# Copies of states with the step moved to the write, the last tokens' features in other PSUM banks, weights turned ahead of a scan, and a new order of 1534 pieces

## The chip, the cores and the metric

The kernel runs on one core of one Trainium2 chip. The time is device microseconds of one launch. PE is the matrix engine (PEld its loads of weights), DVE the vector engine, ACT the scalar engine, POOL the GpSimd engine, SP the engine that issues most DMAs. SBUF is the on-chip memory of 128 partitions; PSUM holds the results of PE in banks of 512 fp32 per partition.

## The reference

The input `x` is (4, 32, 128, 128) in fp32: 4 batches, 32 images ("tokens"), 128 rows `h` of 128 elements. Two layers follow each other; each adds a mixing part and then a recurrent part to `x`. `_ln_c` and `_ln_t` normalise each row of 128.

```python
# --- layer 0 ---
x = x + _L0_conv_ref(_ln_c(x), ...)     # attention over the 32 tokens with spectral convolutions, two mixers
t = _to_tokens(x)                       # (4, 32*128, 128): rows one after the other
t = t + _L0_ffn_ref(_ln_t(t), W, V, gamma, beta)
x = _from_tokens(t, x)
# --- layer 1 ---
x = x + _L1_conv_ref(_ln_c(x), bias, up_filter, dn_filter)
t = _to_tokens(x)
t = t + _L1_ffn_ref(_ln_t(t), W, V, gamma, beta)
x = _from_tokens(t, x)

def _ffn_ref(x, W, V, gamma, beta):     # the same for both layers
    Wx = einsum('bti,hi->bth', x, W)    # then batch norm over all B*T rows
    y[t] = sigmoid(Wx[t] + y[t-1] @ V.T)    # a scan over the 4096 rows of a batch

def _L1_conv_ref(x, bias, up, dn):      # every image by itself
    x = x + bias                        # one per token
    x = repeat(x, 2, both axes); x = conv_same(x, up)    # 12 x 12 taps, separable
    x = leaky_relu(x, 0.2) * sqrt(2)
    x = conv_same(x, dn)[::2, ::2]
```

## The kernel before

`XA` [128 rows h, batch, token, 128 w] holds the images in SBUF throughout. `WX` holds, for each group of 8 tokens, `[h, (token, batch)]` columns with the 128 features on the partitions: first the products `W x`, then the states of the recurrence. The program has these stages, with their place in the profiled execution: the attention of layer 0 (0 to about 240 us), the mixers and the products of the first recurrence (to 485), the scan of layer 0 (485 to 541), the convolution of layer 1 together with what surrounds it (541 to 835), and the scan of layer 1 with the output (835 to 911).

**The recurrences.** `Recurrence(layer, ...)` turns its two 128x128 weights on PE when it is made (`ps_wt`, L408 and L409), and `prepare()` copies them to SBUF (L414). While tokens are multiplied (`ps_wx`, L446), DVE takes bn_stats of each product (L449) and ACT copies it to `WX` (L1671). `scan()` first combines these statistics (`bn_aggr`, L1895; POOL's power, L360; L1898, L1899) and then goes over the rows: the 32 tokens and 5 pieces of 26 rows of each are run side by side from a guessed state with 12 warming steps, each step a product (L1912), a DVE addition (L1913) and a sigmoid on ACT (L1914). `f0.check()` (`CK` in the list below) compares the ends of pieces with the starts of the next ones; a second, sequential program stands behind a flag for the case that they differ, and is not run here.

**The convolution stage** is one list of 1534 names, `CONVOLUTIONS`, written out in the source. A loop issues the pieces in the order of the list, and `in_order` ties the instructions of PE, DVE, ACT, POOL and SP to that order on each engine. So the list sets which work stands behind which on an engine; between engines only data and buffers make one wait for another. A piece is a name and a token `t` (0 to 31), with a batch where it has `t.b`, or a unit `u` (0 to 63: half a token, two batches):

- `YC t`: ACT copies the states of token t out of `WX` to `yc` (L2099); `Ya t`, `Yb t`: PE turns them in two rounds to `ps_y`; `A t`: DVE adds them to `XA` (L2102).
- `CS t`: row statistics for the norm ahead of the convolution (DVE, L385); `CN`, `CP`, `CO q`: for a group of tokens the variance (DVE, L2013 to L2018), its power on POOL (L2025), the shifts (DVE, L2031, L2036); `X t.b`: the normalised image `XN` (POOL, L2045; DVE and ACT, L2042, for tokens 0 and 1).
- `Ra u`, `Rb u`: PE filters up along one axis into `ps_r`; `Q u`: ACT copies to `q`; `Ka u`, `Kb u`: the other axis into `ps_k`; `La u`, `Lb u`: ACT copies to `raw` (L2172); `Va u`, `Vb u`: DVE's leaky relu to `U` (L2180).
- `D u`: PE filters `U` of unit u down one axis into `ps_d` (L2190) and the copied result of unit u-1 down the other into `ps_e` (L2197); `C u` and `E u`: ACT's copies of the two; `AD u`: the sum to `XA`, on POOL for odd u below 58 and on DVE for the others (L2213).
- `FS t`: row statistics of the finished token (DVE, L385) and a DMA of it to DRAM (`turned`, SP, L2118); `FN`, `FP`, `FO q`: as `CN`, `CP`, `CO`; `N t.b`: the normalised image `xn` (POOL; DVE and ACT for tokens 30 and 31); `Ta t`, `Tb t`: turned on PE into `ps_x`; `TC t`: ACT's copy to `xt` (L2131); `M t`: the products with W of the second recurrence into `ps_w` (PE, L2136); `PS t`: their bn_stats (DVE, L2140); `PC t`: ACT's copy to `WX` (L2144).

A pass with an `a` and a `b` part uses PE's quarters; the `b` part waits for a no-operation on SP (L2072) that waits for the `a` part, so SP's queue, with the DMAs of `FS`, stands between them. PSUM is shared out as `ps_r` one tile of two banks, `ps_d` one bank, `ps_e` one bank, and `ps_k` two tiles of two banks for `Y`, `K`, `T` and `M`. Of `yc`, `xn` and `xt` there are two buffers, of `XN` three. At the end of the stage DMAs read `turned` back into `XA` in another order (L2244, L2247), ahead of the output of the second scan.

## Time and profile before

| | |
|---|---|
| three runs | 911.6, 914.01, 912.22 us; median 912.22 |
| profiled execution | 912.8 us; span of its instructions 911.0 us |
| busy share of the span | PE 89%, PEld 67%, DVE 80%, ACT 74%, POOL 40% |
| mean granted clock of PE | 0.946 |
| first scan, 485 to 541 us | PE busy 52.30 of 56.00, clock 1.00 |
| start of the convolution stage, 541 to 560 us | PE busy 14.28 of 19.00, clock 0.55 |
| its middle, 560 to 815 us | PE busy 247.48 of 255.00, DVE 197.01, ACT 201.61, POOL 198.21, clock 1.00 |
| its end, 815 to 836 us | PE busy 16.87 of 21.00, clock 0.92 |

All durations are of one profiled execution. A group line gives the source line, engine, operation, output and input tiles with their shapes, the count, then the busy time in us and the mean in ns, then the idle time of the engine ahead of these instructions and what ended it. A timeline line gives the start and the length in us of one instruction, or of several that follow each other, and in brackets the idle time before it with its releaser.

### The profile page before, as it was taken

Reading aid. Unit: us, or ns where it says so; the run is one execution under the profiler, and the core shown is the slowest. Engines: PE = TensorE matmul, PEld = TensorE weight load, DVE = VectorE, ACT = ScalarE, POOL = GpSimd, SP = SyncE. Lnnn points to the kernel's source line nnn. Section 1 sums busy time; section 2 is a strip of 40 time slices with the busy share of each in tenths; the row PEclk is TensorE's granted clock in tenths of the full one; section 3 lists DMA queues with packets and bytes.
Section 4 is the critical chain, followed back from the end, with each engine's and each line's share of the span. In section 5 each row is a group of like instructions: output and inputs, shape, how many; then the busy total and the mean of one; then the engine's idle time right before and its main releaser. Section 6 shows DMA issues by size and latency. Waiting matters only on the chain.

```text
span 911.0 us, 31218 instructions
## 1 busy us (share of the span) xinstructions
PE 806.4 (89%) x12678; PEld 608.0 (67%) x12678; DVE 728.3 (80%) x2352; ACT 670.1 (74%) x1644; POOL 364.1 (40%) x605
## 2 busy tenths in 40 slices
PE   2999969998796899999778988999999999997994
PEld 2656557568673465555436986888878888884994
DVE  5997477778667889989988988887777787666996
ACT  2774636565672879998788996888778787775995
POOL 2000000003142554344521003687977977962253
PEclk9999979997767999999999997999999999999997
DMA  9906000000101101102100000111111111118354
GB/s 228 240 4 124 1 1 1 1 1 1 48 1 47 47 25 47 48 25 70 47 1 1 1 1 3 39 39 38 39 28 38 31 35 40 38 39 306 123 180 151
DMA packets 69419, 49.67 MB, mean 55 GB/s; under 512 B 4561, under 2 KB 64465, under 8 KB 69201
## 3 DMA queue, kind: packets, MB, share of 16 engines
q1 hardware_dynamic: 68929, 47.31, 18.2%
q8 instruction: 102, 1.67, 0.8%
q0 software_dynamic: 288, 0.01, 0.2%
q14 instruction: 52, 0.43, 0.2%
q10 hardware_dynamic: 48, 0.26, 0.1%
HBM read 30.68 MB, written 16.88 MB: 52 GB/s over the span
## 4 chain that ended last, share of the span: by engine, by line
PE 40%; DVE 24%; ACT 11%; POOL 8%; issue 4%; DMA 0%; DVEq 0%; SPq 0%; ACTq 0%; POOLq 0%
PE ps_k L2066 5%; PE ps_d L2190 4%; DVE XA L1584 4%; DVE XA L1583 4%; ACT WXY L1914 3%; PE ps_scan L1912 3%; ACT yw L1914 3%; PE ps_y L1303 3%; PE ps_r L2066 2%; PE pm L1055 2%; PE ps_w L2136 2%; PE ps_e L2197 2%; PE ps_st L1426 2%; PE ps_inv L481 2%; POOL c_r L2025 2%
## 5 line engine op out<-in xcount | busy, mean ns | idle before, releaser
L1913 DVE SCALAR_TENSOR_TENSOR ps_scan<-WXY,bs,ps_scan 128x128 f32<-128x128 f32 x376 | 104.8, 351 | 1.3 <-PE ps_scan L1912 0.8
L2180 DVE SCALAR_TENSOR_TENSOR U<-raw 128x512 f32<-128x512 f32 x128 | 87.5, 701 | 20.2 <-ACT raw L2172 19.9
L2066 PE MATMUL ps_k<-WXY,q 64*64 64x134 f32 x2048 | 86.7, 283 | 0.4
L2172 ACT COPY raw<-ps_k 128x512 f32<-128x512 f32 x128 | 73.3, 595 | 13.5 <-PE ps_k L2066 11.3
L2190 PEld LDWEIGHTS ps_d<-WXY,U 128*64 128x64 f32 x2048 | 67.4, 137 | 20.2 <-issue 14.4
L2045 POOL TENSOR_SCALAR XN<-XA,c_r,c_o 128x128 f32<-128x128 f32 x120 | 78.1, 664 | 1.2 <-PE ps_k L2066 0.7
L2190 PE MATMUL ps_d<-WXY,U 128*64 128x67 f32 x2048 | 73.4, 224 | 0.5 <-DVE U L2180 0.4
L2045 POOL TENSOR_SCALAR xn<-XA,f_r,f_o 128x128 f32<-128x128 f32 x120 | 62.8, 534 | 17.3 <-PE ps_x L2066 14.0
L2066 PEld LDWEIGHTS ps_k<-WXY,q 64*64 64x64 f32 x2048 | 60.7, 135 | 6.7 <-ACT raw L2172 1.1
L2066 PE MATMUL ps_r<-WXY,XN 64*64 64x134 f32 x1024 | 57.3, 285 | 5.5 <-POOL XN L2045 2.6
L850 PE MATMUL ps_st<-cst,XA 128*128 128x130 f32 x256 | 43.5, 310 | 14.3 <-ACT XA L833 11.2
L1641 ACT ACTIVATE xn<-XA,f_o,f_r 128x128 f32<-128x128 f32 x120 | 50.9, 489 | 4.7 <-DVE f_o L1623 4.6
L1420 ACT ACTIVATE Z<-Z,k,aB 128x128 f32<-128x128 f32 x128 | 51.1, 481 | 3.4 <-DVE Z L1415 3.2
L850 PEld LDWEIGHTS ps_st<-cst,XA 128*128 128x128 f32 x256 | 35.2, 206 | 27.4 <-ACT XA L833 12.3
L1583 DVE SCALAR_TENSOR_TENSOR XA<-ps_inv,r1B,xin 128x128 f32<-128x128 f32 x128 | 44.0, 344 | 8.7 <-PE ps_inv L1576 8.7
L1584 DVE SCALAR_TENSOR_TENSOR XA<-Z,gB,XA 128x128 f32<-128x128 f32 x128 | 46.5, 363 | 5.0
L2025 POOL TENSOR_TENSOR c_r<-c_e,neg_half 128x16 f32<-128x16 f32 (+2 forms) x10 | 25.8, 2582 | 52.6 <-DVE c_e L2018 52.5
L496 PE MATMUL ps_inv<-invq,cst 64*128 64x512 f32 x128 | 41.9, 685 | 4.5 <-ACT invq L487 3.8
L2158 ACT COPY q<-ps_r 128x512 f32<-128x512 f32 x64 | 37.9, 591 | 8.6 <-PE ps_r L2066 8.3
L1290 DVE TENSOR_TENSOR df<-WXY 128x1088 f32<-128x1088 f32 x32 | 40.2, 1286 | 2.1 <-PE ps_y L1303 2.1
L2197 PE MATMUL ps_e<-WXY,q 128*64 128x67 f32 x1024 | 40.8, 222 | 0.0
L446 PE MATMUL ps_wx<-xt,wvt 128*128 128x512 f32 x64 | 35.6, 640 | 5.8 <-ACT WXY L453 4.5
(459 smaller groups left out, 2249.0 us busy)
## 6 DMA issues: line engine op xcount, KB each, us to landing
XA<-in_x_dram SPq DMA_DIRECT2D x16, 512.0 KB, 7.3
xin<-in_x_dram SPq DMA_DIRECT2D x32, 256.0 KB, 3.3
turned<-XA SPq DMA_DIRECT2D x32, 256.0 KB, 2.5
out_dram<-res SPq DMA_DIRECT2D x52, 128.0 KB, 2.1
XA<-turned SPq DMA_DIRECT2D x6, 1024.0 KB, 9.5
WXY<-dd SPq DMA_DIRECT2D x4, 544.0 KB, 11.1
XA<-turned SPq DMA_DIRECT2D x6, 256.0 KB, 7.3
out_dram<-resl SPq DMA_DIRECT2D x12, 128.0 KB, 2.1
```

What stands on the lines that cost most here:

```text
L850: mm(p[:, i, :], XA[:, b, t0 + j + i, :], cst[:, C_E : C_E + 130], start=True, stop=True)
L1420: nc.scalar.activation(z, z, AF.Gelu, bias=k1, scale=aB[:, j : j + 1])
L1583: stt(a, p2[c, b][:, i], r1B[:, j : j + 1], xin[c, b - b % 2][:, b % 2, i], ALU.mult, ALU.add)
L1584: stt(a, Z[c][:, b, i], gB[c][:, n : n + 1], a, ALU.mult, ALU.add)
L1913: stt(p4, WX[:, :, h, :], s[:, 0:1], p4, ALU.mult, ALU.add)
L1914: nc.scalar.activation(dst, p4, AF.Sigmoid, bias=s[:, 1:2])
L2045: e.tensor_scalar(dst, src_, r, o, ALU.mult, ALU.add)
L2066: m = mm(dst, data, taps, start=(n == 0 and (i, j) not in last), stop=(n == 1), skip_group_check=True)
L2172: nc.scalar.copy(raw[u, k], banks["k", u][:, k])
L2180: stt(U[u][:, k].rearrange("p k s m -> p (k s m)"), v, SLOPE, v, ALU.mult, ALU.max)
L2190: mm(p[HALVES[s], m, b, REACH[k]], U[v][:, b, k, s, HALVES[m]], DR[:, k, REACH[k]], start=(m == 0 and b == 0 and k == 0), stop=(k == 1), s ...
L2197: mm(p[HALVES[j], b * P : b * P + P][:, REACH[m]], q3[v - 1][:, m, b, HALVES[j]], DC[:, m, REACH[m]], start=(b == 0 and m == 0), stop=(m = ...
```

## The change

Four things are changed. The first three are small:

```diff
-        f0.scan()
         with tc.tile_pool(name="ps_f", bufs=1, space=PSUM) as ps_f:
             f1 = Recurrence(1, xtp, wk, ps_f, ps_f)
             f1.prepare()
+        f0.scan()
-        H2 = NB // 2
+        H2, LATE = NB // 2, NT - 4
...
-                            banks[name, u] = pool.tile([P, 2, 4 * P], F32, tag="x", name=f"ps_{name}")
+                            banks[name, u] = pool(u).tile([P, 2, 4 * P], F32, tag="x", name=f"ps_{name}")
...
             def state_columns(t):
                 yc[t] = cv.tile([P, NB, P], F32, tag="yc", name="yc")
                 j = t % TP * NB
-                nc.scalar.copy(yc[t], WX[:, t // TP, :, j : j + NB].rearrange("p h b -> p b h"))
+                nc.scalar.copy(yc[t].rearrange("p b h -> p h b"), WX[:, t // TP, :, j : j + NB])
...
             def feature_products(t):
-                p = banks["w", t] = ps_k.tile([P, 2, 4 * P], F32, tag="x", name="ps_w")[:, 0]
+                if t < LATE:
+                    p = ps_k.tile([P, 2, 4 * P], F32, tag="x", name="ps_w")[:, 0]
+                elif t % 2:
+                    p = ps_d.tile([P, 2, H2, P], F32, tag="d", name="ps_w").rearrange("p m b h -> p (m b h)")
+                else:
+                    p = ps_e.tile([P, 4 * P], F32, tag="e", name="ps_w")
+                banks["w", t] = p
...
-                ("Y", "y", ps_k, turned_by(lambda t, w, b, h: yc[t][w, b, h])),
-                ("T", "x", ps_k, turned_by(lambda t, h, b, w: xn[t][h, b, w])),
-                ("R", "r", ps_r, up_rows), ("K", "k", ps_k, up_cols),
+                ("Y", "y", lambda t: ps_k, turned_by(lambda t, w, b, h: yc[t][w, b, h])),
+                ("T", "x", lambda t: ps_r if t >= LATE and t % 2 else ps_k, turned_by(lambda t, h, b, w: xn[t][h, b, w])),
+                ("R", "r", lambda u: ps_r, up_rows), ("K", "k", lambda u: ps_k, up_cols),
```

1. `YC` goes through `WX` in the order in which it is stored: it reads runs of 4 elements (16 bytes) at a step of 32 elements and writes to `yc` with a step of 128 elements. Before, it read single elements at a step of 32 and wrote runs of 128.
2. The products of tokens 28 to 31 go to the banks of `ps_d` (odd tokens) and `ps_e` (even ones), and the turns of tokens 29 and 31 to `ps_r`, in place of `ps_k`.
3. The second recurrence's weights are turned and copied ahead of the first scan. On PE the two transposes then stand between the last two groups of products of the first recurrence; on DVE the copy stands ahead of the `bn_aggr` that begins the scan.
4. `CONVOLUTIONS` is another order of the same 1534 pieces. It begins and ends like this:

```diff
-YC0 YC1 Ya0 Ya1 Yb0 Yb1 YC2 A0 YC3 A1 Ya2 CS0 Yb2 Ya3 YC4 A2 Yb3 CN0 YC5 Ya4 Yb4 CS1 CP0 YC7 A3 CO0 Ya5 CN1 Yb5 X0.0
-YC6 CP1 CS2 X0.1 X0.3 X0.2 Ra0 CO1 CS3 Rb0 Q0 A4 Ra1 CN2 Ka0 Rb1 X1.0 Kb0 CP2 Q1 A5 X1.3 X1.2 La0 Ka1 CS4 Lb0 Ra3
-CO2 Kb1 X1.1 Va0 Ya6 X2.0 Rb3 X3.0 CS5 Yb6 Q3 X2.3 La1 Vb0 X2.1 Ra2 X2.2 Va1 Rb2 Lb1 X3.2 D0 A6 Q2 X3.1 X3.3 Vb1 Ka2
-C0 CK Ra4 Kb2 D1 La2 Lb2 Va2 Ka3 E0 C1 Rb4 AD0 Kb3 Vb2 Ya7 CS6 Q4 D2 La3 Lb3 Va3 Ra5 E1 Vb3 Ka4 C2 AD1 Yb7 Rb5 YC8
+YC1 Ya1 YC0 Ya0 Yb1 A1 Yb0 A0 CS0 CN0 CP0 CS1 YC3 Ya3 Yb3 A3 YC2 Ya2 Yb2 CO0 X0.0 X0.1 YC4 X0.3 Ra0 CN1 A2 YC5 Ya4
+X0.2 CS2 CP1 CO1 Rb0 Q0 X1.0 X1.3 X1.1 Yb4 A4 X1.2 Ra1 Ka0 YC6 CS3 CN2 CP2 Rb1 Kb0 CS4 Q1 La0 Va0 Lb0 Ra3 Ka1 Vb0
+CO2 X2.0 X2.1 Rb3 Ya5 Kb1 Q3 La1 Lb1 Ra2 Yb5 A5 X3.0 X3.2 Rb2 D0 Q2 Ya6 Ka2 X3.3 X3.1 C0 Va1 Ra4 Vb1 Yb6 A6 CS6 YC7
+Kb2 La2 Lb2 Va2 Vb2 D1 C1 Ka3 Ya7 CS5 E0 Rb4 Kb3 La3 Lb3 Va3 Q4 Yb7 D2 Ka4 X2.3 X2.2 C2 Ra5 YC8 Kb4 A7 Vb3 Rb5 E1
...
-Vb63 Ta25 E61 Ta26 C62 AD61 Tb25 Tb26 TC25 N28.0 FS30 D63 N27.0 TC26 N28.1 FN8 N28.3 M25 N28.2 E62 C63 N27.3 AD62
-N27.2 Ta28 PC25 N27.1 D64 PS25 FP8 Tb28 E63 TC28 AD63 M26 N29.0 FO8 FS31 N29.2 M28 PC26 N29.1 FN9 N29.3 PC28 PS26
-FP9 PS28 Ta27 FO9 Tb27 Ta29 TC27 N30.0 N30.1 Tb29 N30.2 M27 N31.0 TC29 N31.1 N31.3 N31.2 M29 PS27 N30.3 PC27 PS29
-Ta30 PC29 Tb30 Ta31 TC30 Tb31 M30 TC31 M31 PC30 PS30 PC31 PS31
+C61 Tb26 La63 FP7 FO7 N28.0 Va63 Lb63 D62 Ta25 Tb25 N28.1 TC26 N27.0 N27.1 N28.2 N27.2 Vb63 E61 AD61 FS30 M26 PS26
+FN8 C62 TC25 M25 PC25 PC26 D63 E62 N28.3 Ta28 Tb28 AD62 N27.3 N29.0 N29.3 PS25 C63 D64 N29.2 TC28 Ta27 E63 AD63 FS31
+FN9 N29.1 M28 Tb27 TC27 PC28 Ta29 Tb29 TC29 FP8 FO8 N30.0 N30.1 M27 N30.2 N30.3 FP9 FO9 N31.0 N31.1 N31.2 N31.3 M29
+PS29 Ta30 Tb30 TC30 PS28 PC29 Ta31 Tb31 M30 PS30 TC31 PC27 M31 PC31 PS27 PC30 PS31
```

In the lines left out the pieces of a unit still follow each other in the same sequence; the distances between the producers (`X`, `N`, `AD`) and their users are others, and `CK` has moved from before `D1` to behind `D6`.

## The prediction

> **What bounds the kernel now.** I read the slices of the span first, then a table of stretches, the groups of instructions, and the timeline at the three places that the change touches. The slices put the convolution stage at 541 to 835 us (slices 24 to 37). The table gives, for each stretch, its length, the busy time of PE, PEld, DVE, ACT and POOL, the granted clock, the DMA share and GB/s:

> ```profile
> 541.00:560.00 19.00, 14.28 (x306) 10.98 (x308) 13.38 (x59) 11.86 (x16) 6.76 (x10) 0.55 0.01 3
> 600.00:625.00 25.00, 24.03 (x764) 20.35 (x754) 20.04 (x57) 19.84 (x38) 24.76 (x37) 1.00 0.12 36
> 725.00:750.00 25.00, 24.70 (x790) 21.05 (x788) 20.29 (x64) 20.61 (x40) 18.16 (x24) 1.00 0.13 35
> 825.00:838.00 13.00, 9.38 (x134) 4.30 (x125) 5.94 (x15) 6.16 (x13) 0.55 (x1) 0.87 1.02 372
> ```

> In the middle PE is busy 24.0 to 24.7 of 25 us and everything else about 20 (POOL once 24.8): PE bounds it, and an order can only take away its few gaps or add some. Idle PE time lies at the two ends: the ramp until the first `D`, at half clock, and the tail behind the last one, `D63` at 816.63. So the ends decide what can be won, and the middle what can be lost.

> **The stepped write.** These are ACT's groups (busy time, mean ns of one):

> ```profile
> L2099 ACT COPY yc<-WXY 128x512 f32<-128x512 f32 x32 | 35.1, 1108 | 7.5 <-PE ps_y L2066 7.5
> L1057 ACT COPY XA<-pm 128x512 f32<-128x512 f32 x20 | 21.2, 1059 | 17.7 <-PE pm L1055 17.7
> L872 ACT COPY WXY<-ps_pr 128x512 f32<-128x512 f32 x8 | 8.3, 1032 | 6.7 <-PE ps_pr L870 6.7
> L2144 ACT COPY WXY<-ps_w 128x512 f32<-128x512 f32 x32 | 18.8, 587 | 11.3 <-DVE bn L2140 9.1 <-PE ps_w L2136 2.1
> ```

> `YC` (L2099) reads with an inner step of 32 elements and writes contiguously. The new form reads 16-byte runs and writes with a step of 128. L1057 and L872 write with that step and cost 1059 and 1032; L2144, which writes 16-byte runs, costs 587, so runs of four are free and a step is not. The new copy is nearest to L1057: 1.06 us, 32 x 0.05 = 1.6 us of ACT in all, off the path: 0. The bounds are 0.59 (16.6 us of ACT freed) and 1.11. [...]

> **The weights ahead of the scan.** At 540.74 the two transposes (L408, L409) and the copy L414 run while PE waits for the first `YC` anyway (PE resumes at 541.84, DVE's next work is at 544.01). Taking them away gains 0. They go to the end of the stage before:

> ```profile
> 484.44 0.30 PEld L446 LDWEIGHTS ps_wx<-xt,wvt 128*128 128x128 f32 x2 [0.79 <-ACT WXY L1671]
> 485.61 0.70 DVE L449 BATCH_NORM_STATS2 bn<-ps_wx 128x6 f32<-128x512 f32 x1 [0.39 <-PE ps_wx L446]
> 486.41 1.02 DVE L1895 BATCH_NORM_AGGREGATE mv<-bn 128x2 f32<-128x192 f32 x1
> ```

> On PE they stand between the last two groups of products; the last bn_stats, the aggregate, POOL's power and the first step of the scan (488.56) follow in one chain. The two take about 0.3 us each with 0.15 of overlap, so the last product is 0.4 us later; the copy of 0.42 fits DVE's idle 0.39 ahead of 485.61. I take +0.4, between 0 (they fit PE's idle 0.79 after the wait for ACT) and 0.9 (transposes and copy in series).

> **The ramp.** Unit 0's first product on `X0.1` now waits for less: before, `X0.1` (on ACT) stands behind eight `YC`, after it stands behind four, close after `CO0`:

> ```profile
> 550.99 0.30 PEld L2066 LDWEIGHTS ps_r<-WXY,XN 64*64 64x64 f32 x4
> 551.40 1.07 ACT L2099 COPY yc<-WXY 128x512 f32<-128x512 f32 x1 [0.68 <-PE ps_y L2066]
> 552.37 0.88 ACT L2042 ACTIVATE XN<-XA,c_o,c_r 128x128 f32<-128x128 f32 x2
> 552.91 0.29 PEld L2066 LDWEIGHTS ps_r<-WXY,XN 64*64 64x64 f32 x4 [1.62 <-ACT XN L2042]
> ```

> `Ra0` can then start at about 549.75 and end without the stop of 1.62. That is 1.4 us earlier for `D0`, which stands at 562.3, but 0.5 us of PE work at full clock (about twice that at the clock of 0.55 here) that came first now follows it. So PE gets about -0.9, within 1.5 either way.

> **The tail.** `D63` starts at 816.63 and the last `PS31` ends at 835.30: 18.67 us. Rows with what ended the idle time before them:

> ```profile
> 824.11 0.32 PEld L2066 LDWEIGHTS ps_x<-ident,xn 64*64 64x64 f32 x16 [2.53 <-DVE bn L2140]
> 826.11 3.48 PE L2136 MATMUL ps_w<-xt,wvt 128*64 128x512 f32 x8
> 829.52 0.32 PEld L2066 LDWEIGHTS ps_x<-ident,xn 64*64 64x64 f32 x16 [1.41 <-ACT WXY L2144]
> 834.60 0.70 DVE L2140 BATCH_NORM_STATS2 bn<-ps_w 128x6 f32<-128x512 f32 x1 [0.16 <-ACT WXY L2144]
> ```

> Twice a turn on PE waits for a bank of `ps_k` whose statistics (DVE) or copy (ACT) are late. In the new code features of tokens 28 to 31 lie in `ps_d` and `ps_e`, the turns of 29 and 31 in `ps_r`: these waits go. Next late is the chain of token 31 itself, by the rows of this trace: `D63` to the end of `AD63` 4.4 (816.63 to 821.00), bn_stats 0.9, `FN9` 1.2, POOL's power with its hand-over 1.15, `FO9` 0.2, `N31` 0.65, both parts of `T31` 0.95, `TC31` 0.6, `M31` 0.95, `PC31` 0.6, `PS31` 0.75, and five changes of engine of 0.14: 13.05. Where the clock is halved, as at 826.11 (8 products in 3.48 us, against 1.94 at 831.99), `M30` and `M31` add 1.8: 14.85. `M25` and `M26` (2 x 0.91) now stand ahead of `D63`. So the gain is 18.67 - 13.05 - 1.82 = 3.8, or 2.0 at half clock; I take 3.0. It could be 0, were the new banks held as long as the old.

> [...]

> **The middle.** The PE work per unit is equal in both lists, some 4 us from `D` to `D`. What differs is how far ahead the producers stand. Taken as distances in PE work along the list, from the last `X` image of a unit to its `Ra` the median falls from 9.6 to 3.3 us, and from `N` to `Ta` from 7.4 to 0.7. `FS` (DVE, and its DMA on SP, behind which the SP release of a turn's second part queues) directly follows POOL's `AD` in 11 places. The trace of before has such stalls, few of them (total, times, longest):

> ```profile
> DVE f_st L385 <- POOL XA L2213: 12.0, 10, 2.1
> PEld ps_r L2066 <- POOL XN L2045: 3.3, 3, 1.3
> ```

> But the lists bind each engine only by itself, and neighbours on different engines need not meet in time: POOL is busy 75% of this stage and can run ahead as far as three `XN` and two `xn` buffers let it. `CK` now stands behind `D6` on DVE, about 1 us ahead of `V7`, against `D1` in the ramp before. At the places walked by hand waits shift by less than 1 us and of both signs. I take 0, within -5 and +9; the upper end is the shortages read literally, next.

> **Sum.** The profiled execution took 912.8 (span 911.0 and 1.8 around it), 0.6 above the median of 912.22. 912.8 - 0.9 - 3.0 + 0.4 + 0 + 0 = 909.3; less the 0.6, 908.7. A measurement of this kernel tells 0.3%, 2.7 us, from no change.

> **Rivals.** *Producers too late (slower).* Wherever the list's lead is shorter than the producer's row (0.664 for an `XN` image, 0.534 for `xn`, 0.727 for POOL's `AD`), PE stops for the rest: summed over the list 1.9 us before, 10.7 after, so +8.8 and 908.7 + 8.8 = 917.5. For it: three such stalls stand in the trace, POOL is busy 24.8 of 25 us at 600, and in the new list POOL has 20.0 us in the four units before `D52`, where PE has 15.4. Against it: POOL's slack over the whole stage. It decides once more than 6.2 of the 8.8 come true (3.5 only cancel the gains). *The step is free.* If ACT takes 0.59 per `YC`, the copies ahead of unit 0 (four or five) shorten the ramp by 2.5: 906.2, and less where the freed ACT also ends the 4.0 us in which PE waits for `xt`: 902.2. Against it stands L1057. *The tail keeps its time:* PE's banks come free, but DVE and ACT do the same statistics and copies one by one behind `N30` and `N31`, and the wait moves to them: 911.7.

> **Chances.** Forecast 0.45 (own range 904 to 912; within it 0.35 faster, 0.10 same). Late producers 0.33 (0.30 slower, 0.03 same or less). Free step 0.12, faster. Tail kept 0.10 (0.05 same, 0.03 faster, 0.02 slower). That makes 0.50 faster, 0.18 same, 0.32 slower. The range goes from 902.5 (free step with its second gain) to 918 (all the shortages, 0.5 over).

> **What would show it.** Right: `yc` near 1060 ns; `D0` near 561.4 with the stage beginning 0.4 later; last `D` to last statistics below 15 us without waits of `ps_x` for `bn` or WXY; PE idle in the middle as before. Wrong: PE's waits in the middle for `XN`, `xn` or SP's release above 5 us together, `yc` near 600 ns, or a tail of 16 us and more with DVE or ACT busy through it.

## The result and the profile after

The changed kernel takes 907.54 us (median of 6 runs, 906.81 to 908.87) against 911.91 for the kernel before (6 runs): a ratio of 0.9948 with the 95% interval [0.9932, 0.9963]. The profiled execution went from 912.8 to 908.87 us, its span from 911.0 to 907.1.

The same stretches as before, in the same columns (length, busy us of PE, PEld, DVE, ACT and POOL, granted clock, DMA share, GB/s):

```profile
541.00:560.00 19.00, 14.53 (x368) 12.08 (x372) 14.40 (x59) 12.97 (x20) 5.68 (x7) 0.64 0.02 4
600.00:625.00 25.00, 24.17 (x792) 20.99 (x785) 19.54 (x55) 19.96 (x39) 20.62 (x30) 1.00 0.12 36
725.00:750.00 25.00, 24.86 (x784) 20.55 (x780) 20.43 (x62) 19.71 (x40) 20.42 (x27) 1.00 0.17 46
825.00:838.00 13.00, 9.56 (x95) 7.54 (x95) 9.70 (x28) 8.11 (x22) 0.55 (x1) 0.87 1.02 371
```

The middle is as full as it was (24.17 and 24.86 of 25 us). In the first 19 us PE's clock is 0.64 in place of 0.55, and 368 products are done in place of 306. ACT's copies of states and of features, by group:

```profile
L2098 ACT COPY yc<-WXY 128x512 f32<-128x512 f32 x32 | 35.4, 1127 | 1.3 <-PE ps_y L2065 1.3
L2149 ACT COPY WXY<-ps_w 128x512 f32<-128x512 f32 x32 | 19.0, 601 | 8.5 <-DVE bn L2145 4.4 <-PE ps_w L2141 4.0
```

The new copy is no faster: 1127 ns after 1108. The timeline of the ramp, up to the first `D`:

```profile
549.40 0.50 PEld L2065 LDWEIGHTS ps_r<-WXY,XN 64*64 64x64 f32 x8 [1.49 <-DVE XN L2044]
551.80 0.58 ACT L2163 COPY q<-ps_r 128x512 f32<-128x512 f32 x1
558.66 1.15 PE L2195 MATMUL ps_d<-WXY,U 128*64 128x67 f32 x32
```

Both halves of `Ra0` run in one piece at 549.40, and `D0` starts at 558.66, 17.74 us behind the first copy of states (540.92); before it was 21.58. The timeline of the tail, from `D63` to the aggregate of the second scan:

```profile
816.51 1.10 PE L2195 MATMUL ps_d<-WXY,U 128*64 128x67 f32 x32
824.53 1.28 PE L2065 MATMUL ps_x<-ident,xn 64*64 64x64 f32 x48
826.45 1.95 PE L2141 MATMUL ps_w<-xt,wvt 128*64 128x512 f32 x8
829.06 0.70 DVE L2145 BATCH_NORM_STATS2 bn<-ps_w 128x6 f32<-128x512 f32 x1 [0.19 <-ACT WXY L2149]
829.79 1.02 DVE L1895 BATCH_NORM_AGGREGATE mv<-bn 128x2 f32<-128x192 f32 x1
```

No turn waits for a bank any more, the eight products take 1.95 us (full clock), and the last `PS31` ends 13.25 us behind the start of `D63`; it was 18.67. But 5.4 us less in the tail and 3.8 in the ramp do not make 3.9 in all, so the stages have to be laid side by side. The table gives distances in us between starts in the profiled executions, for the two kernels and the experiments below; "half" is the number of half-clock periods of 3.41 us in the ramp, in the tail and at the start of the second scan.

| | first copy to `D0` | `D4` to `D56` | `D56` to 2nd aggregate | 2nd aggregate to end | 1st aggregate to end | half |
|---|---|---|---|---|---|---|
| before | 21.58 | 215.37 | 43.97 | 75.67 | 424.59 | 5, 1, 0 |
| changed | 17.74 | 216.25 | 40.92 | 77.28 | 420.47 | 4, 0, 1 |
| yc_read_step | 17.74 | 215.68 | 41.09 | 77.38 | 420.18 | 4, 0, 1 |
| weights_after_scan | 17.66 | 216.01 | 40.76 | 77.45 | 420.15 | 4, 0, 1 |
| banks_alone | 21.50 | 215.97 | 40.56 | 77.18 | 423.24 | 5, 0, 1 |
| tail_and_banks | 21.72 | 216.01 | 41.02 | 76.85 | 423.63 | 5, 0, 1 |
| ramp_alone | 16.66 | 221.78 | 43.65 | 76.99 | 427.35 | 3, 1, 1 |
| middle_alone | 21.73 | 217.71 | 45.59 | 75.12 | 428.13 | 5, 1, 0 |
| old_middle | 17.69 | 220.37 | 40.73 | 76.39 | 423.45 | 4, 0, 1 |
| fill_ramp | 16.08 | 215.75 | 40.96 | 75.83 | 417.24 | 0, 0, 0 |
| fill_scan | 17.75 | 215.82 | 40.93 | 76.23 | 419.02 | 4, 0, 0 |
| before_fill_ramp | 20.56 | 215.62 | 42.33 | 75.88 | 422.55 | 1, 0, 0 |
| check_split | 17.73 | 216.62 | 40.19 | 76.31 | 419.13 | 4, 0, 1 |
| together | 16.07 | 216.56 | 40.74 | 75.28 | 417.27 | 0, 0, 0 |

For the change itself: ramp -3.84, `D0` to `D4` +0.26, `D4` to `D56` +0.88, tail -3.05, second scan +1.61. That is -4.14, and the column from the first aggregate to the end gives -4.12; with 0.2 more ahead of that aggregate it is the -3.9 of the spans. (What lies ahead of the first aggregate varies between executions from 483.5 to 487.3 us and the change adds nothing there (weights_after_scan), so the column from there to the end is the cleanest comparison of profiles.)

The +1.61 is in no sum of the prediction. These are the first microseconds of the second scan, 3 to 7 and 7 to 12 us behind its aggregate, first in the kernel before, then in the changed one:

```profile
838.33:842.33 4.00, 3.94 (x30) 3.92 (x30) 4.00 (x16) 4.00 (x17) 0.00 (x0) 1.00 1.05 387
842.33:847.33 5.00, 5.00 (x39) 4.97 (x39) 5.00 (x20) 5.00 (x20) 0.00 (x0) 1.00 1.01 359
```

```profile
832.79:836.79 4.00, 3.93 (x20) 3.94 (x21) 3.29 (x11) 3.42 (x12) 0.00 (x0) 0.57 1.05 393
836.79:841.79 5.00, 5.00 (x39) 4.91 (x38) 5.00 (x20) 5.00 (x20) 0.00 (x0) 1.00 1.05 387
```

PE gets 0.57 of its clock and does 20 products in place of 30; afterwards both run alike. In the kernel before one such period lay in the tail (826.11, eight products in 3.48 us), in the changed one it lies here. In this execution, as in the other thirteen, the clock changes only at points 3.41 us apart (the last section has the figures). This is the period ahead of the slow one, from 829.49 on, in the changed kernel:

```profile
829.49:832.91 3.42, 1.44 (x11) 1.25 (x11) 2.65 (x10) 0.50 (x3) 0.55 (x1) 1.00 1.04 386
```

PE's wait of 1.91 us for the scan's first states (830.95 to 832.86) lies wholly in it, and PE is busy for 1.44 us of it.

### The profile page after: what moved, and what is told of

Its sections match the earlier page's. It is cut to its first block, busy times and chain, and to the rows that moved or that the text cites. A ratio compares the mean times of both kernels' runs of the same rounds, so it can differ in the third digit from the quotient of the medians.

```text
span 907.1 us, 31233 instructions
## 1 busy us (share of the span) xinstructions
PE 807.2 (89%) x12678; PEld 608.8 (67%) x12678; DVE 734.7 (81%) x2352; ACT 666.8 (74%) x1644; POOL 365.2 (40%) x605
## 3 DMA queue, kind: packets, MB, share of 16 engines
q1 hardware_dynamic: 68929, 47.31, 18.5%
## 4 chain that ended last, share of the span: by engine, by line
PE 42%; DVE 23%; ACT 11%; POOL 7%; issue 4%; SPq 0%; DVEq 0%; ACTq 0%; POOLq 0%
PE ps_scan L1912 5%; PE ps_k L2065 5%; PE ps_d L2195 4%; DVE XA L1584 4%; DVE XA L1583 4%; ACT WXY L1914 3%; PE ps_y L1303 3%; PE ps_r L2065 2%; PE pm L1055 2%; POOL XN L2044 2%; PE ps_inv L481 2%; PE ps_e L2202 2%; PE ps_st L1426 2%; PE ps_w L2141 2%; ACT yw L1914 2%
## 5 line engine op out<-in xcount | busy, mean ns | idle before, releaser
L2185 DVE SCALAR_TENSOR_TENSOR U<-raw 128x512 f32<-128x512 f32 x128 | 89.6, 728 | 27.9 <-ACT raw L2177 27.6
L2177 ACT COPY raw<-ps_k 128x512 f32<-128x512 f32 x128 | 71.1, 599 | 17.7 <-PE ps_k L2065 15.0
L2044 POOL TENSOR_SCALAR xn<-XA,f_r,f_o 128x128 f32<-128x128 f32 x120 | 68.3, 578 | 18.7 <-PE ps_x L2065 14.0
L2044 POOL TENSOR_SCALAR XN<-XA,c_r,c_o 128x128 f32<-128x128 f32 x120 | 73.6, 622 | 5.0 <-issue 2.3
L446 PE MATMUL ps_wx<-xt,wvt 128*128 128x512 f32 x64 | 35.6, 639 | 5.8 <-ACT WXY L453 4.5
```

The costliest lines, as they stand in the source:

```text
L2044: e.tensor_scalar(dst, src_, r, o, ALU.mult, ALU.add)
L2177: nc.scalar.copy(raw[u, k], banks["k", u][:, k])
L2185: stt(U[u][:, k].rearrange("p k s m -> p (k s m)"), v, SLOPE, v, ALU.mult, ALU.max)
```

## The experiments

Each run was compared with runs of the kernel before on the same chip. Single runs of one kernel spread over up to 5 us, so effects below 1 us are read from the table.

**yc_read_step**: the changed kernel with the old copy.

```diff
-                nc.scalar.copy(yc[t].rearrange("p b h -> p h b"), WX[:, t // TP, :, j : j + NB])
+                nc.scalar.copy(yc[t], WX[:, t // TP, :, j : j + NB].rearrange("p h b -> p b h"))
```

> The changed kernel with the old copy of states (read with a step, write in storage order); all else as changed. Theory (the stepped write is no gain): a copy goes from 1.127 us back to about 1.108, 32 x 0.02 = 0.6 us of ACT off the path, so 907.5 within 0.5. Rival (the stepped write slows its neighbours in SBUF: DVE's leaky relu was 0.701 us before and is 0.728 in the changed kernel): that group goes back to 0.70 and the middle of the stage is up to 1.7 us shorter, 905.8.

Measured: 908.92 us, ratio 0.996 [0.9945, 0.9976]; the changed kernel has 0.9948 [0.9932, 0.9963]. A copy takes 1.112 us, DVE's leaky relu 0.735 as in the changed kernel (0.728), so its growth from 0.701 is not the copies' doing. From the first aggregate to the end 420.18 against 420.47: this edit is worth nothing.

**weights_after_scan**: the changed kernel with the weights turned behind the scan.

```diff
+        f0.scan()
         with tc.tile_pool(name="ps_f", bufs=1, space=PSUM) as ps_f:
             f1 = Recurrence(1, xtp, wk, ps_f, ps_f)
             f1.prepare()
-        f0.scan()
```

> The changed kernel with the second recurrence's weights turned after the first scan again. Theory: the aggregate at the start of the first scan is back from 486.60 to 486.41 and nothing is lost at the start of the convolution stage, since PE waits there for the first copy of states: -0.2, 907.3. Rival (PE's two transposes and DVE's copy stand ahead of the first turn and its addition, and the first turn begins later): +0.3, 907.8.

Measured: 908.59 us, ratio 0.9951 [0.9933, 0.9968]; first copy to `D0` 17.66. From ACT's last copy of `xt` ahead of the scan to the aggregate it is 3.17 us here, 3.10 in the changed kernel and 3.16 in the one before. The edit costs nothing at either place.

**banks_alone**: the kernel before with the new banks only (the edits of `in_rounds`, `feature_products` and the table of passes, `LATE = NT - 4`).

> The kernel before with only the other PSUM banks for tokens 28 to 31 (old order, old copies, old place of the weights). Theory (half of the tail's gain is the two waits for banks of ps_k): the waits of 2.53 and 1.41 us on PE go, the last D to the last statistics shrinks from 18.67 to about 16, and the time goes from 911.9 to 909.5. Rival (in the old order the statistics and copies behind them are late by themselves, the banks only move the wait): 18.67 stays within 0.7, 911.9.

Measured: 911.64 us, ratio 0.9991 [0.9981, 1.0001]. Its timeline in the tail:

```profile
821.45 1.28 PE L2064 MATMUL ps_x<-ident,xn 64*64 64x64 f32 x48
823.79 1.94 PE L2140 MATMUL ps_w<-xt,wvt 128*64 128x512 f32 x8
825.65 0.32 PEld L2064 LDWEIGHTS ps_x<-ident,xn 64*64 64x64 f32 x16 [0.81 <-DVE bn L2144]
830.97 1.02 DVE L1894 BATCH_NORM_AGGREGATE mv<-bn 128x2 f32<-128x192 f32 x1
```

Both waits for banks are gone: the 0.81 in the third line is idle time of the weight loads alone, PE's own products run from 823.79 without a gap into those of 825.66. And `D56` to the second aggregate falls by 3.4 us in the old order, more than the 3.05 of the changed kernel. Part of it is clock: before_fill_ramp below has the old banks and no half-clock period in the tail, and there the stretch is 42.33. So the period costs 1.6 and the banks give 1.8. PE's own lines in the kernel before say the same:

```profile
824.11 1.28 PE L2066 MATMUL ps_x<-ident,xn 64*64 64x64 f32 x48 [1.65 <-DVE bn L2140]
829.53 1.05 PE L2066 MATMUL ps_x<-ident,xn 64*64 64x64 f32 x32
```

The 2.53 and 1.41 us of the prediction stand on lines of weight loads. PE itself was idle for 1.65 us ahead of the first of these turns and not at all ahead of the second, where the products at half clock ran until 829.59. Of the 3.4 the second scan then gives back 1.5: its start has the half-clock period now, and the middle of this execution is 0.6 longer. That is why the time moves so little.

**tail_and_banks**: the kernel before with the new banks, and the list taken from the old order up to `D56` and from the new one behind it.

> The kernel before with the other banks, and with the old order up to the piece D56 and the rest in the new order; ramp, middle, copies and weights of before. Theory (places add up): last D to last statistics is 13.2 us with two token products more ahead of it, so 3.6 us less than before: 908.3. Rival (the new tail needs the new middle ahead of it): images and sums that the old order has further behind are late for it, the tail is over 15 us: 910.5.

Measured: 912.42 us, ratio 0.9997 [0.9984, 1.0009]. The tail did as the theory said (`D63` to the aggregate 13.56, and 41.02 from `D56`), so the rival is wrong, but it is no better than with the banks alone (40.56), and the second scan again takes 1.2 us more. I had expected 908.3, 3.6 less than before; the profile shows 1.0 less. The difference is 1.2 in the second scan, 0.6 in the middle and 0.65 from `D56` on. The median of the runs, 912.42, lies 1.8 above the profiled execution, and nothing here explains that.

**ramp_alone**: the kernel before with the new order up to `D4`. The seam of the list:

```diff
-... A8 Lb5 D4 YC10 Va5 CS8 Ka6 E3 C4 Vb5 ...
+... A8 Lb5 Rb7 Q7 D4 CK YC9 AD2 YC10 Va5 CS8 Ka6 E3 C4 Vb5 ...
```

> The kernel before with the new order up to the piece D4 and the rest in the old order; old banks, copies and weights. Theory (the ramp's gain is its own): the first copy of states to D0 takes 17.7 us in place of 21.6, PE is at half clock for four periods of 3.41 us (13.65) in place of five (17.07), and nothing later changes, so the time goes from 912.5 to 908.7. Rival (the ramp only borrows: work that the old order did ahead of D0 now follows, and the old order behind the seam meets it late): D0 to D62 grows from 251.6 by 2 us or more, 910.7.

Measured: 913.98 us, ratio 1.0004 [0.9994, 1.0014]. The ramp is even shorter (16.66), but 6.4 us are lost behind the seam, 6.0 of them between `D4` and `D6` (13.2 us against 7.2 before). The old order has the check of the first scan (`CK`) ahead of `D1`, the new one behind `D6`, so the splice puts it right behind `D4`. DVE's and PE's lines there, and a stretch behind them:

```profile
571.75 0.88 DVE L1958 TENSOR_TENSOR d<-WXY 128x128 f32<-128x128 f32 x4
573.53 1.02 DVE L1960 TENSOR_SCALAR d<-d 128x640 f32<-128x640 f32 x1
576.49 0.71 PE L2189 MATMUL ps_d<-WXY,U 128*64 128x67 f32 x8 [3.36 <-DVE U L2179]
577.00:579.00 2.00, 1.43 (x26) 1.24 (x25) 2.00 (x7) 0.61 (x2) 2.00 (x3) 0.50 0.33 96
```

The check fills DVE from 571.5 to 575.4, the leaky relu of unit 5 stands behind it, PE waits 3.36 us, and two periods of half clock follow the wait. So the gain of the ramp is its own, and the seam shows what a badly placed check costs: more than the ramp wins.

**middle_alone** and **old_middle**: the kernel before with only `D4` to `D56` in the new order, and the changed kernel with only these in the old order.

> The kernel before with only the pieces between D4 and D56 in the new order. Theory (the new middle costs a little): D4 to D56 goes from 215.4 to 216.3 us as in the changed kernel, and the time from 912.5 to 913.4. Rival (producers too late, as in the rival of the prediction, hidden in the changed kernel by its better ramp): D4 to D56 is 3 us longer or more, 915.5. Rival (no cost at all, the 0.9 was given back from the ramp): 215.4, 912.5.

> The changed kernel with the pieces between D4 and D56 in the old order. Theory: D4 to D56 goes from 216.3 back to 215.4, all else as changed: 0.9 less than the changed kernel, some 3.9 + 0.9 = 4.8 below the kernel before. Rival (the pieces behind D56 are made for the new middle): D56 to D62 grows from 23.3 by more than 0.9, and nothing is won.

Measured: 916.21 us, ratio 1.0032 [1.0021, 1.0044], and 912.17 us, ratio 0.9987 [0.9978, 0.9997]. Neither theory nor rival fits: both splices lose at their seams. middle_alone takes 8.3 us from `D4` to `D6`, where the changed kernel takes 5.9, and 1.6 more from `D56` to `D62` than the kernel before; old_middle has the check behind `D4` like ramp_alone and a PE wait of 3.25 us there. What the middle by itself costs is better read from whole lists: `D4` to `D56` is 215.37 to 216.01 in the four executions with the old order (mean 215.74) and 215.68 to 216.25 in the five with the new one and the check in one piece (mean 215.90). That is no difference.

**fill_ramp**: the changed kernel with products on PE that nothing reads, where PE waits in the ramp.

```diff
+                if piece[0] == "W":        # W8 ahead of Ya1, W3 Ya0, W6 Ya3, W4 Ya2, W14 Ra0
...
+                    for j in range(int(piece[1:])):
+                        nc.tensor.transpose(p[:, j % 4 * P : j % 4 * P + P], ident, ident)
```

> The changed kernel with 35 products more on PE that nothing reads (128x128 turns of the identity into free banks), placed where PE waits at the start of the convolution stage: 8 ahead of Ya1, 3 ahead of Ya0, 6 ahead of Ya3, 4 ahead of Ya2, 14 ahead of Ra0. Theory (the half clock in the ramp follows from PE's waits there, and costs time): fewer than four periods of half clock of 3.41 us, the first copy of states to D0 falls from 17.7 to about 15.2 us, 2.5 us less in all. Rival (the ramp is bound by the copies, additions and statistics, and the clock is only seen there): D0 within 0.5 of before. Rival (the added products delay the turns themselves): D0 up to 1.5 us later.

Measured: 905.34 us, ratio 0.992 [0.9907, 0.9933]. Stretches from 540 to 555 us:

```profile
540.00:545.00 5.00, 4.70 (x115) 3.63 (x113) 2.50 (x10) 3.56 (x4) 0.00 (x0) 1.00 0.01 3
545.00:550.00 5.00, 4.21 (x96) 3.17 (x94) 4.79 (x24) 2.71 (x5) 2.03 (x2) 1.00 0.02 7
550.00:555.00 5.00, 3.96 (x127) 3.24 (x131) 4.83 (x21) 4.55 (x10) 1.64 (x1) 1.00 0.02 3
```

The half clock is gone from the whole ramp, and `D0` comes 1.66 us sooner, less than the 2.5 expected. A likely reason is DVE, busy 4.8 of 5 us from 545 on here and 4.7 to 4.8 in the same microseconds of the changed kernel; no run tests it.

The second scan has no half-clock period either here and is 1.45 us shorter, though no product was added there and PE's two waits are the same (1.17 and 1.91 us). What differs is where they fall between the points at which the clock changes:

```profile
824.69:828.11 3.42, 1.91 (x14) 1.19 (x10) 2.87 (x5) 1.07 (x2) 0.21 (x1) 1.00 1.04 376
828.11:831.52 3.41, 1.84 (x14) 1.84 (x14) 3.00 (x13) 2.26 (x9) 0.34 (x1) 1.00 1.05 391
```

The point at 828.11 divides the second wait, PE is busy for 1.91 us of the one period (56%) and 1.84 of the other (54%), and the clock stays at 1.00. So the 1.45 us come from where the second scan falls between these points, not from products at that place. Nor does the shorter tail decide it: ramp_alone, with the tail of before, has a slow period in the tail and another at the scan.

**before_fill_ramp**: the same in the old order.

```diff
+# W8 ahead of Ya0, W3 Ya1, W6 Ya2, W3 Ya3, W2 Ya4, W4 Ra0, W5 Ka0
```

> The kernel before with 31 products that nothing reads where its PE waits in the ramp (8 ahead of Ya0, 3 ahead of Ya1, 6 ahead of Ya2, 3 ahead of Ya3, 2 ahead of Ya4, 4 ahead of Ra0, 5 ahead of Ka0). Theory (some 2 of the 3.8 us that the new order wins in the ramp are the half-clock period that it saves, the rest is order): the first copy of states to D0 falls from 21.6 to about 18.5, still above the 16.1 of the new order with such products. Rival (it is all clock): 16.5. Rival (it is all order): 21 or more.

Measured: 912.45 us, ratio 1.0 [0.999, 1.001]. Four of five half-clock periods in the ramp go, but `D0` comes only 1.0 us sooner: between the theory (18.5) and "all order" (21 or more). With hardly any half clock in either, the two orders stand at 20.56 and 16.08. The added products were once in their own way: `Q0`'s copy ends at 552.85, but five of them run from 553.53 to 554.85 ahead of `Ka0`, so up to 1.2 of the 20.56 may be theirs. Four slow periods fewer thus won 1.0 to 2.2 us here, and 1.66 in fill_ramp, some 0.3 to 0.6 each. The changed kernel has one fewer than the kernel before, so its ramp's gain of 3.84 is mostly order, and the clock is a second effect.

**fill_scan**: the changed kernel with 13 such products behind the first five of the second scan, and nothing else.

```diff
+                        if k == 0 and warm is not None:
+                            warm(self.product)      # 13 turns of the identity, behind that product
```

> The changed kernel with 13 products that nothing reads on PE behind the first five products of the second scan, where PE waits 1.9 us for the statistics. Theory (the shorter tail moved a half-clock period of 3.41 us from the tail to the first steps of the scan): the scan runs its first steps at full clock, its aggregate to the end takes 75.8 us in place of 77.3, and some 1.4 us are won in all. Rival (the slower first steps come from the DMAs that read the tokens back, at 1.04 of their share in these microseconds): 77.3 stays.

Measured: 905.74 us, ratio 0.9924 [0.991, 0.9938]. The same microseconds of the scan as above:

```profile
832.78:836.78 4.00, 3.91 (x29) 3.90 (x30) 4.00 (x16) 4.00 (x17) 0.00 (x0) 1.00 1.05 396
836.78:841.78 5.00, 5.00 (x40) 4.99 (x39) 5.00 (x20) 5.00 (x20) 0.00 (x0) 1.00 1.05 387
```

The clock is full and PE does 29 products, with the same DMA traffic beside it; the rival with the DMAs is wrong. The stretch to the end is 76.23, the first scan's aggregate to the end 1.45 us shorter. Half clock at the start of the scan did cost the changed kernel part of its gain: over all executions in the table the stretch is 76.98 us on the mean of the eight with it and 75.67 on that of the six without. The theory's reason, the shorter tail, does not decide by itself. Of the executions with nothing added at the scan, seven of the eight with the new banks have the slow period there (not fill_ramp), and one of the four with the old ones (ramp_alone).

**check_split**: the changed kernel with the check in five pieces (`CK` behind `D6` becomes `CK0`, and `CK1` to `CK4` stand behind `Vb7` to `Vb10`).

> The changed kernel with the check of the first scan (3.7 us of DVE in one piece behind D6) cut into five pieces behind D6, V7, V8, V9 and V10. Theory (PE is late by 0.9 us at D8 because the leaky relu of unit 7 stands behind the whole check): D6 to D8 goes from 7.7 to 6.9 us and the rest of the stage is as before, 0.8 less in all. Rival (DVE makes up for it later anyway, PE waits at another place): D4 to D56 within 0.3 of the 216.3 of the changed kernel.

Measured: 907.47 us, ratio 0.9947 [0.9934, 0.9961], the changed kernel's own. `D6` to `D8` falls from 7.73 to 6.59 us, but `D8` to `D10` grows by 1.5: the rival is right, what is won is lost again at another place.

**together**: both groups of added products and the split check.

> The changed kernel with both groups of added products and the check cut up. Theory: what each wins adds up, as they lie at different places: 1.7 in the ramp, 1.4 at the scan, 0.8 behind D6, 3.9 less than the changed kernel (first aggregate to the end 416.6 in place of 420.5), about 8 less than the kernel before. Rival (with the added products in the ramp the scan's start has lost its half-clock period already, as the run with products in the ramp alone showed): 1.7 + 0.8 = 2.5 less than the changed kernel, 418.0.

Measured: 905.78 us, ratio 0.992 [0.9907, 0.9934], 417.27 from the first aggregate to the end. That is fill_ramp's 417.24. It lies between the theory's 416.6 and the rival's 418.0 and decides for neither by its size; but as fill_ramp already had full clock at the scan, the products added there could win nothing more, which was the rival's point, and the split adds nothing here either. The three kernels in the new order with added products are the fastest of all, some 2 us below the changed one. They are equal to each other within their intervals, and these just touch that of the changed kernel.

## Why the prediction was right, and where not

The time (908.7 forecast, 907.54 measured) and its sign came out, and the main reason held, that the ends decide and not the middle. Term by term:

- **The stepped write**: 1.06 us forecast, 0 on the path; 1127 ns measured, just above the upper bound of 1.11, and 0 on the path by yc_read_step. The read in runs with a stepped write (1127 ns) won nothing over the stepped read with a write in order (1112), and ACT's copies of features, which write in runs of 16 bytes, take 601 ns.
- **The weights ahead of the scan**: +0.4 forecast, 0 measured. That is the lower of the two bounds: from the start of PE's last four products to their end it is 2.22 us with the two transposes among them and 2.21 without.
- **The ramp**: -0.9 forecast, -3.84 measured. The step that failed is "That is 1.4 us earlier for `D0`". It has both gains in its rows, the start of `Ra0` (550.99 to 549.75) and the stop of 1.62 inside it, but they add up to 2.9: `Q0` stands 10.9 us behind the first copy in place of 13.8, 2.9 sooner. And the work that I charged for being moved behind `D0` (a token's turn and half a row product more between `D0` and `D4`) cost 0.26. The half-clock period saved, which I had not counted, is the smaller part by before_fill_ramp.
- **The tail**: -3.0 forecast, -3.05 measured from `D56` on. `D63` to the last statistics was forecast at 13.05 to 14.85 and is 13.25, at full clock. banks_alone shows that the waits for banks were the right place. That the new order adds nothing to them I had not foreseen. The near hit is luck in part: by the runs the banks give 1.8, the half-clock period that left the tail 1.6, and the new order takes 0.4 back. Its "waits of PE" of 2.53 and 1.41 us were idle time of the weight loads; PE's own were 1.65 and 0.
- **The middle**: 0 forecast with -5 to +9; +0.9 in the two profiles, 0.2 on the mean of several. The rival of late producers did not come. Waits of PE's weight loads and of DVE in the changed kernel between 562 and 816 us (total, times, longest):

```profile
PEld ps_r L2065 <- POOL XN L2044: 2.1, 4, 0.8
PEld ps_x L2065 <- SPq L2071: 1.5, 3, 1.0
DVE f_st L385 <- POOL XA L2218: 0.2, 1, 0.2
```

  The first was 3.3 and the last 12.0; PE's own waits for `XN` are 0.5 us in place of 2.6. The shortages counted along the list (10.7 us) were for the most part no waits. That POOL runs ahead of the list's neighbours on other engines would explain it; no run shows that by itself.
- **Not in the sum**: the half clock at the start of the second scan, +1.6. It and what these two profiles have more in the middle (+0.9) and between `D0` and `D4` (+0.3) cancel the 2.9 by which the ramp was undersized. That the total came out so near is luck; the sign and the places are not.

## What to carry to other kernels

Where one engine is full through a long stage, look for the gain at its two ends, and add up every wait that the first unit loses there: they stood in series here, where the earlier start of `Ra0` and its stop of 1.62 us made 2.9. Where a wait is taken from a stage end, look at the granted clock of the next stage as well: the same wait of PE (1.91 us) was followed by a period of half clock in the changed kernel, where one period held all of it (PE busy 42%), and not in fill_ramp, where two shared it (56% and 54%). 13 products that nothing reads, put into it, won 1.1 us of the second scan in the trace and some 2 us by the ratios. And where a line of weight loads shows idle time, look at PE's own line before counting it as a wait of PE (2.53 and 1.41 us were 1.65 and 0 here). Pieces of an order made as a whole cannot be judged by splicing, unless one looks at what the seam itself puts together.
